# A warm-up for TensorE, and half of the slot inputs turned by VectorE and a trip through DRAM

## The chip, the cores and the metric

The kernel runs on one core of one Trainium2 chip. A core has five engines that run side by side and wait for each other by semaphores: TensorE (PE in the profile; PEld is its weight load), VectorE (DVE), ScalarE (ACT), GpSimd (POOL) and SyncE (SP), which here issues all the DMAs. All data is float32. The metric is the device time of one execution in microseconds. Before the change the median of three runs is 435.57 us (434.58 to 435.74).

## The reference, cut to what matters

Two batches of 1024 tokens with 256 features pass through four blocks, each added to its input: an attention on a short context, a grouped feed-forward, a second attention with sigmoid weights, and a soft mixture of experts with 8 experts of 128 slots (1024 slots in all). The change touches the start of the program and the last block:

```python
xn = rms_norm(x, gamma_x)
se = rms_norm(slot_embeds, gamma_slot)
logits = jnp.einsum('bsd,etd->bset', xn, se)
dispatch = jax.nn.softmax(logits, axis=1)
slots = jnp.einsum('bsd,bset->betd', xn, dispatch)
h = jax.nn.gelu(slots @ w1, approximate=False)
processed = h @ w2
combine = jax.nn.softmax(logits.reshape(b, s, e * t), axis=-1)
out = jnp.einsum('bnd,bsn->bsd', processed.reshape(b, e * t, d), combine)
```

The slots are a weighted mean of the tokens for each slot (`dispatch`), the experts are one two-layer network on each slot, and `combine` brings the results back to the tokens.

## The kernel before, in words

The program is written with tiles whose waits a framework places. Parts under `tc.manual_schedule` keep the order of the text on the engines named (`IN_ORDER` is DVE and PE); elsewhere a scheduler with its own estimates orders each engine, and `keep_in_program_order` pins single instructions to their place in the text. Every DMA is issued by SP, in one order, and each DMA takes the next of eight semaphores, so that one cannot be issued before the DMA eight places ahead of it has landed.

**Start.** SP loads the first group of feed-forward weights in five pieces (`load_group(0, (1, 1, 2, 2, 2))`, L802), and PE multiplies the two weight matrices of the group with each other (`product(0)`, L820: 16 matmuls, 32 records of the trace, since a float32 matmul leaves two). Meanwhile POOL fills the constants: `ident`, `ones`, zeros, and the biases' `b2z`. Then come the key and value products of the first attention (`pk`, `pv`, `pwk`, `pvw`), and for each quarter of the tokens `weigh(q)` (scores `psc`, softmax on DVE and ACT) and `attend(q)` (L1056: PE turns the weights, `pat`, ACT copies them to `atT`, PE multiplies, `po`).

**Gather.** For each batch b, `gather(b, c)` (L398) sums the tokens for the 128 slots of chunk c, c from 0 to 7: 8 matmuls into a PSUM bank (`psl`, L390), the last column of which is the sum of weights. DVE takes its reciprocal (`rz`, L409) and scales the chunk (`sl`, L411). `turn_slots(b, c)` has PE turn the chunk, two transposes of 128x128 against `ident` (`pst`, L420), so that features lie on partitions; for each pair of chunks `slots_out` (L427) has DVE copy the turned pair out of PSUM and scale it by gamma_x (L428, one instruction for each half of the features) into `slT`. Seven of the eight turns stand in the gather, one chunk late; the last stands in `hidden`.

**Turns of the exponentials.** The combine step needs the exponentials `ec` with slots on partitions. `turn(q, h)` (L279) turns half of them for a quarter q of the tokens: four DVE transposes of 32x32 squares (L297) into `tr`, then 16 DMAs (L306) that put the squares in their places, back into `ec`. Batch 0 has the quarters 0 and 1, batch 1 the quarters 2 and 3. Before, turns (0,0), (0,1) and (1,0) stand in the gather of batch 0 at c = 1, 2 and 6, turn (1,1) in `processed(0)`, and the four of batch 1 in its gather at c = 0, 2, 4 and 6. In the gather of batch 0 DVE also has three of the eight additions `less` (L376), the rest of which POOL does.

**Hidden, processed, combined.** `hidden(b)` (L470) multiplies `slT` by w1 by Strassen's scheme in Winograd's form, with seven products of 512-column quadrants for each j from 0 to 3 (`pmh`, L476). Its right sides are sums of quadrants of `slT` made by `sum_slots` (L450); its left sides were made by POOL in `sum_weights` (L438) in the memory that held `seT`. The products go through eight PSUM banks; DVE adds them (L517 to L533), ACT applies the Gelu (L486). `processed` (`pp`) and `combined` (`pc`) are further such schemes, both through L547. `first_sums` of batch 1 stands in `processed(1)` and is the first reader of the turned `ec` there.

The same trip by way of DRAM that the change uses is already there as `turned_by_square` (L155): DVE transposes by squares (L134), one DMA of 512 KB writes them to DRAM, four DMAs of 128 KB bring them back to their places (L159, L161). It turns the slot embeddings and the inputs of the second attention, and `in_order` (L166) views such a tile with its columns in order.

Of the kernel before, what the change touches and what calls it, by code (L numbers as in the profile page):

```python
# [9 lines left out]
FP = mybir.dt.float32  # L10
AF = mybir.ActivationFunctionType
ALU = mybir.AluOpType
# [3 lines left out]
P = 128  # L16
B = 2
S = 1024
D = 256
# [33 lines left out]
def tile_kernel(  # L53
# [29 lines left out]
    def bank(name, side=0):  # L83
        return ps[side].tile([P, 512], FP, tag="bank", name=name)

    ident = const.tile([P, P], FP, name="ident")
    make_identity(nc, ident)
    ones = const.tile([P, P], FP, name="ones")
    nc.gpsimd.memset(ones, 1.0)
    zero = const.tile([P, 1], FP, name="zero")  # L90
    nc.gpsimd.memset(zero, 0.0)

# [30 lines left out]
    def transposed(src, dst, name, side=0, out=nc.any.tensor_copy):  # L123

        for c in range(DC):
# [2 lines left out]
                nc.tensor.transpose(pt[:, ts(t, P)], src[:, t, ts(c, P)], ident)  # L128
            out(dst[:, c, :], pt)

    def squares(src, tr, late=False):

        for t in range(QT):
            turn = nc.vector.transpose(  # L134
                tr[:, :, :, t, :].rearrange("p r c n -> p c r n"),
                src[:, t, 0:D].rearrange("p (c r n) -> p c r n", c=DC, r=R4),
            )
            if late:
                tc.keep_in_program_order(turn)

# [14 lines left out]
    def turned_by_square(src, dst, tr, name, late=False):  # L155

        squares(src, tr, late)
        by_row = dram.tile([P, R4, DC * QN // R4], FP, name=f"d_{name}")
# [221 lines left out]

    slTs, prs, pts, sls, hss, m12s = {}, {}, {}, {}, {}, []

    pzs = {}

    def gather_from(b, c, tiles):
        if c not in pzs:
# [11 lines left out]
    def gather(b, c):  # L398

        if b == 0 and c == 0:  # L400

            for tiles in (range(4), range(4, ST)):
                for i in range(3):
                    gather_from(b, i, tiles)
        elif b > 0 or c > 2:
            gather_from(b, c, range(ST))
        pz = pzs.pop(c)
        rz = stat.tile([P, 1], FP, tag="rz", name=f"rz_{b}_{c}")
        nc.vector.reciprocal(rz, pz[:, D : D + 1])  # L409
        sl = pools["m12"].tile([P, D], FP, tag="sl", name=f"sl_{b}_{c}", bufs=2)  # L410
        nc.vector.tensor_scalar(sl, pz[:, 0:D], rz, None, ALU.mult)  # L411
        sls[c] = sl

    def turn_slots(b, c):

        if c % 2 == 0:
            pts[c // 2] = bank(f"pst_{b}_{c // 2}", 1)
        pt = pts[c // 2]
        for dc in range(DC):
            nc.tensor.transpose(  # L420
                pt[:, ds(dc * 2 * P + (c % 2) * P, P)], sls[c][:, ts(dc, P)], ident
            )
        if c % 2 and c < EC - 1:
            for dc in range(DC):
                slots_out(b, c // 2, dc)

    def slots_out(b, c2, dc):  # L427
        nc.vector.tensor_scalar(  # L428
            slTs[b][:, dc, ts(c2, 2 * P)], pts[c2][:, ts(dc, 2 * P)], gx[:, dc : dc + 1],
            None, ALU.mult,  # L430
        )


# [4 lines left out]
    def sum_weights():  # L438
        m1s = m12s[0]
        a11, a12 = m1s[:, 0, 0:512], m1s[:, 1, 0:512]  # L440
        a21, a22 = m1s[:, 0, 512:], m1s[:, 1, 512:]
        st = const.tile([P, DC, NSLOT], FP, tag="seT", name="m1_sums")
        s1, s2, s4 = st[:, 0, 0:512], st[:, 0, 512:], st[:, 1, 0:512]
        nc.gpsimd.tensor_tensor(s1, a21, a22, ALU.add)
        nc.gpsimd.tensor_tensor(a21, a11, a21, ALU.subtract)
        nc.gpsimd.tensor_tensor(s2, s1, a11, ALU.subtract)
        nc.gpsimd.tensor_tensor(s4, a12, s2, ALU.subtract)
        lefts.extend([a11, a12, s4, a22, s1, s2, a21])

    def sum_slots(b):  # L450

        x = slTs[b]
        b11, b12, b21, b22 = x[:, 0, 0:512], x[:, 0, 512:], x[:, 1, 0:512], x[:, 1, 512:]

        t0, t1_ = (
            keep[b].tile([P, QT, XW], FP, tag=f"xh_{i}", name=f"sl_sums_{b}_{i}").rearrange(
                "p t d -> p (t d)"
            )
            for i in range(2)
        )  # L460
        t1, t2, t4 = t0[:, 0:512], t0[:, 512:1024], t1_[:, 0:512]
        slots_out(b, EC // 2 - 1, 0)
        nc.vector.tensor_tensor(t1, b12, b11, ALU.subtract)
        slots_out(b, EC // 2 - 1, 1)
        nc.vector.tensor_tensor(t2, b22, t1, ALU.subtract)
        nc.vector.tensor_tensor(b12, b22, b12, ALU.subtract)
        nc.vector.tensor_tensor(t4, b21, t2, ALU.subtract)
        rights[b] = [b11, b21, b22, t4, t1, t2, b12]

    def hidden(b):  # L470


        def alone(i, j):
            to = bank(f"pmh_{b}_{j}_{i}", nb[0] % 2)
            nb[0] += 1
            nc.tensor.matmul(  # L476
                to,
                lhsT=lefts[i][:, ts(j, P)],
                rhs=slTs[b][:, i, 0:512] if i < 2 else rights[b][i],
                start=True,  # L480
                stop=True,
            )
            return to

        def gelu(h):
            nc.scalar.activation(h, h, AF.Gelu)  # L486

        NU = OC // 2

        with tc.manual_schedule(engines=IN_ORDER):  # L490
            p1s = [alone(0, 0)]
            turn_slots(b, EC - 1)
            p1s.append(alone(0, 1))
            p2 = alone(1, 0)
            sum_slots(b)
        hs = {}

        def begin(j):

            for g in range(2):  # L500
                for u in range(2):
                    fc = j + u * NU
                    if fc % 2 == 0:
                        hss[b, g, fc // 2] = keep[b].tile(
                            [P, 2, 512], FP, tag=f"lg_{4 * g + fc // 2}", name=f"mh_{b}_{g}_{fc}"
                        )
            hs[j] = [
                hss[b, g, (j + u * NU) // 2][:, j % 2, :] for g in range(2) for u in range(2)
            ]
            nc.scalar.copy(hs[j][0], p1s[j])  # L510

        begin(0)
        for j in range(NU):
            h11, h21, h12, h22 = hs[j]
            p5 = alone(4, j)
            p6 = alone(5, j)
            nc.vector.tensor_tensor(h12, h11, p6, ALU.add)  # L517
# [12 lines left out]
            nc.vector.tensor_tensor(h11, h11, p2, ALU.add)  # L530
            gelu(h11)
            p3 = alone(2, j)
            nc.vector.tensor_tensor(h12, h12, p3, ALU.add)  # L533
            gelu(h12)
            if j + 2 < NU:
                p1s.append(alone(0, j + 2))

    nb = [0]

# [220 lines left out]
    with (  # L760
# [135 lines left out]
        with tc.tile_pool(name="p0", bufs=1) as p0, tc.tile_pool(name="a0", bufs=2) as a0:  # L896
# [156 lines left out]
                )  # L1053
                ats[q] = at

            def attend(q):  # L1056
# [5 lines left out]
                nc.scalar.copy(atT, pat)  # L1062
                for i in range(2):
                    po = bank(f"po0_{q}_{i}")
                    for k in range(2):
# [266 lines left out]
    for u in range(1, B * ST + 2):  # L1332
# [24 lines left out]
        ms[:, 0 : DC * FF].rearrange("p (c n) -> p c n", c=DC),  # L1357
        ms[:, DC * FF :].rearrange("p (c n) -> p c n", c=OC),
    ]
    nc.sync.dma_start(out=ms, in_=m12_in)  # L1360
    for b in range(B):
        slTs[b] = pools["slp"].tile([P, DC, NSLOT], FP, tag="slT", name=f"slT_{b}")
        with tc.manual_schedule(engines=(IN_ORDER | {mybir.EngineType.SP}, ACT_ORDER)[b]):
# [93 lines left out]
```

## Time and profile before

| | |
|---|---|
| median of three runs | 435.57 us |
| profiled execution, time / span | 435.35 / 433.5 us |
| PE / DVE / ACT / POOL busy | 423.7 / 335.0 / 111.8 / 81.3 us |
| first matmul starts | 3.83 us |
| gather of batch 0 (`psl`), `hidden(0)` starts | 222.06 us, 251.50 us |
| gather of batch 1, `hidden(1)` starts | 326.05 us, 355.50 us |
| last work on the chain ends | DVE L711, 430.43 us |

The 1.85 us between time and span lie outside the recorded instructions. Times in the text are microseconds from the start of the span. "x32" counts records, and a float32 matmul has two. The list of waits names the engine and line that waited, what released it, the total, the number of times and the longest; the chain of waits follows the work back from the end of the execution; the timeline gives start and duration, and in brackets the idle time before an instruction and what ended it.

### The profile page before, as it was taken

The page shows a single profiled execution, that of the slowest core. Times are in us where ns is not written, and L with a number is a line of the kernel's source. Part 1 is how long each engine was busy: PE and PEld are TensorE (multiplying, and loading weights), DVE is VectorE, ACT ScalarE, POOL GpSimd, SP SyncE. Part 2 cuts the span into 40 slices and gives each one's busy share as a digit, 9 for nine tenths or more (in the row PEclk, how much of TensorE's full clock was granted, in tenths as well). Part 3 has the DMA queues.
Part 4 walks back from the last instruction along what each step waited for, and adds up shares of the span by engine and source line. Part 5 has one row for each costly group of instructions (what it writes and reads, how often), then busy time and mean ns, then how long its engine had stood idle before and what let it go on. Part 6 is the DMA issues. An engine that isn't in the chain of part 4 may idle for free.

```text
span 433.5 us, 6357 instructions
## 1 busy us (share of the span) xinstructions
PE 423.7 (98%) x2328; PEld 314.6 (73%) x2328; DVE 335.0 (77%) x751; ACT 111.8 (26%) x210; POOL 81.3 (19%) x81
## 2 busy tenths in 40 slices
PE   6999999999999999999999999999999999999996
PEld 5778888888644445444468854799998874499996
DVE  0576989899866787998777997995994669795956
ACT  1212143203244441333570536400000003520000
POOL 3011331325122111200886920000000000000000
PEclk9999999999999999999999999999999999999999
DMA  8997496520443432321044664041013666500002
GB/s 276 406 421 301 160 369 271 195 98 2 145 147 105 110 48 30 48 30 21 0 144 126 98 99 73 0 72 28 0 38 81 97 98 91 85 2 1 2 2 98
DMA packets 96641, 47.86 MB, mean 110 GB/s; under 512 B 86625, under 2 KB 91873, under 8 KB 95201
## 3 DMA queue, kind: packets, MB, share of 16 engines
q1 hardware_dynamic: 96610, 47.46, 39.4%
q8 instruction: 18, 0.29, 0.3%
q14 instruction: 13, 0.11, 0.1%
HBM read 31.70 MB, written 5.25 MB: 85 GB/s over the span
## 4 chain that ended last, share of the span: by engine, by line
PE 84%; DVE 11%; POOL 1%; ACT 1%; issue 1%; DMA 1%; DVEq 0%; ACTq 0%
PE psl L390 13%; PE pp L547 12%; PE pc L547 12%; PE pmh L476 11%; PE pmt L820 10%; PE pl L245 7%; PE pq L1204 3%; PE pf L1218 3%; PE po L879 2%; DVE b2z L851 2%; PE psg L1275 2%; PE poT L1307 2%; DVE lg L253 1%; PE psc L1029 1%; DVE hn_f L780 1%
## 5 line engine op out<-in xcount | busy, mean ns | idle before, releaser
L820 PE MATMUL pmt<-wg 128*128 128x256 f32 x256 | 59.8, 392 | 3.8 <-DMA wg<-in_wff_dram 3.8
L390 PE MATMUL psl<-xh,lg 128*128 128x258 f32 x256 | 58.0, 380 | 0.0
L820 PEld LDWEIGHTS pmt<-wg 128*128 128x128 f32 x256 | 50.0, 197 | 10.9 <-DMA wg<-in_wff_dram 3.8
L245 PE MATMUL pl<-seT,xhT 128*128 128x512 f32 x128 | 56.1, 594 | 0.2 <-DVE rmax L264 0.2
L390 PEld LDWEIGHTS psl<-xh,lg 128*128 128x128 f32 x256 | 47.6, 190 | 7.0 <-issue 0.5
L245 PEld LDWEIGHTS pl<-seT,xhT 128*128 128x128 f32 x128 | 24.1, 190 | 29.2 <-issue 25.7
L376 POOL TENSOR_TENSOR lg<-lg,mb 128x1024 f32<-128x1024 f32 x13 | 33.2, 2597 | 26.8 <-ACT mb L192 25.3
L547 PEld LDWEIGHTS pp<-ms,mh 128*128 128x128 f32 x256 | 29.4, 192 | 1.0 <-issue 1.0
L547 PE MATMUL pp<-ms,mh 128*128 128x128 f32 x256 | 29.7, 276 | 0.0
L268 ACT ACTIVATE ec<-lg,nm 128x1024 f32<-128x1024 f32 x16 | 18.4, 1149 | 39.7 <-DVE nm L253 39.7
L851 DVE SCALAR_TENSOR_TENSOR b2z<-wg,fr,b2z 128x256 f32<-128x256 f32 x48 | 24.6, 514 | 0.4
L486 ACT ACTIVATE mh<-mh 128x512 f32<-128x512 f32 x32 | 19.3, 628 | 20.3 <-DVE mh L520 18.7
L476 PE MATMUL pmh<-slT,ms 128*128 128x512 f32 x48 | 24.2, 592 | 0.0
L547 PE MATMUL pp<-m_sums,mh 128*128 128x128 f32 x192 | 22.1, 275 | 0.0
L547 PE MATMUL pc<-pr,ec 128*128 128x128 f32 x192 | 22.1, 275 | 0.0
L547 PEld LDWEIGHTS pp<-m_sums,mh 128*128 128x128 f32 x192 | 21.8, 192 | 0.0
L547 PEld LDWEIGHTS pc<-pr,ec 128*128 128x128 f32 x192 | 21.8, 192 | 0.0
L1284 ACT ACTIVATE sg<-psg 128x512 f32<-128x512 f32 x32 | 16.5, 602 | 18.6 <-PE psg L1275 18.6
L379 ACT ACTIVATE lg<-lg 128x1024 f32<-128x1024 f32 x16 | 16.1, 1045 | 16.6 <-POOL lg L376 16.6
L297 DVE STREAM_TRANSPOSE tr<-ec 128x512 f32<-128x512 f32 x32 | 19.8, 678 | 0.0
L558 DVE TENSOR_TENSOR mh<-mh,mh 128x1024 f32<-128x1024 f32 x16 | 18.5, 1220 | 1.5 <-PE pp L547 1.5
L547 PE MATMUL pc<-pr_sums,ec 128*128 128x128 f32 x160 | 18.5, 275 | 0.0
(189 smaller groups left out, 678.9 us busy)
## 6 DMA issues: line engine op xcount, KB each, us to landing
wg<-in_wff_dram SPq DMA_DIRECT2D x6, 2048.0 KB, 15.0
ec<-tr SPq DMA_DIRECT2D x128, 64.0 KB, 2.3
xT<-in_xT_dram SPq DMA_DIRECT2D x4, 512.0 KB, 13.2
x<-in_x_dram SPq DMA_DIRECT2D x4, 512.0 KB, 14.8
wg<-in_wff_dram SPq DMA_DIRECT2D x2, 1024.0 KB, 11.3
d_a<-tr_a SPq DMA_DIRECT2D x4, 512.0 KB, 2.6
hTa<-d_a SPq DMA_DIRECT2D x16, 128.0 KB, 2.8
xhT<-tr_m SPq DMA_DIRECT2D x64, 32.0 KB, 2.0
```

Of the source, the lines that this page charges most:

```text
L245: nc.tensor.matmul(pl, lhsT=xhTs[q][:, dc, ts(t, P)], rhs=in_order(seT[:, n], dc), start=(dc == 0), stop=(dc == DC - 1),)
L268: nc.scalar.activation(ecs[q][:, :, t, :], lg.rearrange("p (h n) -> p h n", h=2), AF.Exp, bias=nm[:, 1:2], scale=-1.0, accum_out=zcs[b][:, ...
L297: ins = nc.vector.transpose(tr[:, :, :, t, :].rearrange("p r c n -> p c r n"), half[:, t, :].rearrange("p (c r n) -> p c r n", c=EC // 2, ...
L376: engine.tensor_tensor(lgs[b][s], lgs[b][s], mbs[b], ALU.add)
L390: nc.tensor.matmul(pz[:, 0:XW], lhsT=lgs[b][s][:, ts(c, P)], rhs=xhs[b * QB + s // QT][:, s % QT, :], start=(s == 0), stop=(s == ST - 1),)
L476: nc.tensor.matmul(to, lhsT=lefts[i][:, ts(j, P)], rhs=slTs[b][:, i, 0:512] if i < 2 else rights[b][i], start=True, stop=True,)
L486: nc.scalar.activation(h, h, AF.Gelu)
L547: nc.tensor.matmul(to, lhsT=left(k, m), rhs=right[:, k, :], start=(k == 0), stop=(k == QT - 1),)
L558: nc.vector.tensor_tensor(dst, x, y, op)
L820: nc.tensor.matmul(pm[:, ts(hc, D)], lhsT=w1g[:, oc, ts(hc, P)], rhs=w2g[:, oc, :], start=(oc == 0 and hc == 0), stop=(oc == OC - 1 and hc ...
L851: nc.vector.scalar_tensor_tensor(acc, weights[g][1][:, oc, :], b1s[:, g, oc : oc + 1], acc, ALU.mult, ALU.add)
L1284: nc.scalar.activation(sg[:, j, :], psgs[j], AF.Tanh, scale=0.5 * DH1**-0.5)
```

## The change

- `ones` is filled by DVE in place of POOL, ahead of `ident`, and PE begins with seven matmuls `ones` by `ones` of 128x128 into a bank that nobody reads (`busy`).
- For chunks 0 to 3 of each batch `gather` scales by the reciprocal and by gamma in one DVE instruction (gamma_x now lies along the free dimension, `gx_row`, loaded by a DMA of its own into the memory of `m1_sums`), DVE transposes the chunk by squares, and after chunk 3 the four go by way of DRAM into the first half of `slT`. Chunks 4 to 7 are turned by PE as before. `slT` is now two views, the first in the order of squares, and readers of the first half go through `in_order` or `by_square`.
- The turns of the exponentials stand elsewhere: (0,0) and (0,1) at c = 3 and 4, (1,0) in `hidden(0)` after j = 1, and in batch 1 (2,0), (2,1), (3,0), (3,1) at c = 0, 4, 5 and 6. The gather of batch 1 now keeps the text's order on DVE, PE and SP.
- `attend` is split: the turn of the first quarter's weights (`turn_weights(0)`) stands ahead of `weigh(1)`.

```diff
+    ones = const.tile([P, P], FP, name="ones")
+    nc.vector.memset(ones, 1.0)
+    busy = bank("busy")
+    for _ in range(7):
+        nc.tensor.matmul(busy[:, 0:P], lhsT=ones, rhs=ones, start=True, stop=True)
     ident = const.tile([P, P], FP, name="ident")
     make_identity(nc, ident)
-    ones = const.tile([P, P], FP, name="ones")
-    nc.gpsimd.memset(ones, 1.0)
...
+    def square(rows, tr, t):
+        return nc.vector.transpose(
+            tr[:, :, :, t, :].rearrange("p r c n -> p c r n"),
+            rows.rearrange("p (c r n) -> p c r n", c=DC, r=R4),
+        )
...
+        if c >= QT:
+            nc.vector.tensor_scalar(sl, pz[:, 0:D], rz, None, ALU.mult)
+            sls[c] = sl
+            return
+
+        nc.vector.scalar_tensor_tensor(sl, pz[:, 0:D], rz, gx_row[0], ALU.mult, ALU.mult)
+        if c == 0:
+            trs_sl[b] = pools["md"].tile(
+                [P, R4, DC, QT, SQ], FP, tag="rmax", name=f"tr_sl_{b}"
+            )
+        square(sl, trs_sl[b], c)
+        if c == QT - 1:
+            from_squares(trs_sl[b], slTs[b][0], f"sl_{b}")
...
-        if c % 2 and c < EC - 1:
+        if c == EC - 3:
...
-        nc.vector.tensor_tensor(t1, b12, b11, ALU.subtract)
+        nc.vector.tensor_tensor(by_square(t1), by_square(b12), b11, ALU.subtract)
...
-                rhs=slTs[b][:, i, 0:512] if i < 2 else rights[b][i],
+                rhs=in_order(slTs[b][0], i) if i < 2 else rights[b][i],
...
-            nc.vector.tensor_tensor(h12, h11, p6, ALU.add)
+            ins = nc.vector.tensor_tensor(h12, h11, p6, ALU.add)
+            if b == 0 and j == 2:
+                tc.keep_in_program_order(ins)
...
                 p1s.append(alone(0, j + 2))
+            if b == 0 and j == 1:
+                turn(1, 0, True)
...
             product(1)
+            turn_weights(0)
             weigh(1)
             attend(0)
...
+    m1_sums.append(const.tile([P, DC, NSLOT], FP, tag="seT", name="m1_sums"))
+
+    gx_row.append(m1_sums[0][:, 1, 512 : 512 + D])
+    nc.sync.dma_start(out=gx_row[0], in_=gammas[0].partition_broadcast(P))
     nc.sync.dma_start(out=ms, in_=m12_in)
...
-                if c > 0:
+                if c > QT:
                     turn_slots(b, c - 1)
...
-                if b == 0 and c in (1, 2, 6):
-                    turn(c // 4, c // 2 % 2 if c < 4 else 0)
-                if b == 1 and c % 2 == 0:
-                    turn(QB + c // 4, c // 2 % 2, True)
+                if b == 0 and c in (3, 4):
+                    turn(0, c - 3)
+                if b == 1 and c in (0, 4, 5, 6):
+                    turn(*{0: (2, 0), 4: (2, 1), 5: (3, 0), 6: (3, 1)}[c])
```

As built, four other places move: a copy `bs` (128x256, for the first group's bias) goes from ACT to DVE, POOL makes `ident` after it has cleared `b2z`, most of the bias row `pp` of group 0 goes behind `pk` on PE, and in `hidden(0)` at j = 2 DVE's addition of p2 (L530) goes ahead of that of L520.

More of the change, by code (lines that the diff above doesn't have):

```diff
@@ L129, in transposed @@
             out(dst[:, c, :], pt)
+    def square(rows, tr, t):
[3 more added lines that the diff above has]
+        )
     def squares(src, tr, late=False):
         for t in range(QT):
[L134 to L137, printed above, removed]
+            turn = square(src[:, t, 0:D], tr, t)
             if late:
@@ L157, in turned_by_square, with from_squares @@
         squares(src, tr, late)
+        from_squares(tr, dst, name)
+    def from_squares(tr, dst, name):
         by_row = dram.tile([P, R4, DC * QN // R4], FP, name=f"d_{name}")
@@ L381, in tile_kernel @@
     slTs, prs, pts, sls, hss, m12s = {}, {}, {}, {}, {}, []
-    pzs = {}
+    pzs, trs_sl, gx_row, m1_sums = {}, {}, [], []
     def gather_from(b, c, tiles):
@@ L410, in gather @@
         sl = pools["m12"].tile([P, D], FP, tag="sl", name=f"sl_{b}_{c}", bufs=2)
-        nc.vector.tensor_scalar(sl, pz[:, 0:D], rz, None, ALU.mult)
-        sls[c] = sl
+        if c >= QT:
[10 more added lines that the diff above has]
+            from_squares(trs_sl[b], slTs[b][0], f"sl_{b}")
     def turn_slots(b, c):
@@ L428, in slots_out @@
         nc.vector.tensor_scalar(
-            slTs[b][:, dc, ts(c2, 2 * P)], pts[c2][:, ts(dc, 2 * P)], gx[:, dc : dc + 1],
-            None, ALU.mult,
+            slTs[b][1][:, dc, ts(c2 - 2, 2 * P)], pts[c2][:, ts(dc, 2 * P)],
+            gx[:, dc : dc + 1], None, ALU.mult,
         )
@@ L441, in sum_weights @@
         a21, a22 = m1s[:, 0, 512:], m1s[:, 1, 512:]
-        st = const.tile([P, DC, NSLOT], FP, tag="seT", name="m1_sums")
+        st = m1_sums[0]
         s1, s2, s4 = st[:, 0, 0:512], st[:, 0, 512:], st[:, 1, 0:512]
@@ L450, in sum_slots, with by_square @@
     def sum_slots(b):
-        x = slTs[b]
-        b11, b12, b21, b22 = x[:, 0, 0:512], x[:, 0, 512:], x[:, 1, 0:512], x[:, 1, 512:]
+        x, y = slTs[b]
+        b11, b21 = in_order(x, 0), in_order(x, 1)
+        b12, b22 = y[:, 0, :], y[:, 1, :]
+        def by_square(v):
+            return v.rearrange("p (t i n) -> p t i n", t=QT, i=R4)
         t0, t1_ = (
@@ L466, in sum_slots @@
         nc.vector.tensor_tensor(b12, b22, b12, ALU.subtract)
-        nc.vector.tensor_tensor(t4, b21, t2, ALU.subtract)
+        nc.vector.tensor_tensor(by_square(t4), b21, by_square(t2), ALU.subtract)
         rights[b] = [b11, b21, b22, t4, t1, t2, b12]
@@ L1054, in weigh, with turn_weights @@
                 ats[q] = at
-            def attend(q):
+            atTs = {}
+            def turn_weights(q):
                 atf = ats[q].rearrange("p g j -> p (g j)")
@@ L1062, in attend @@
                 nc.scalar.copy(atT, pat)
+                atTs[q] = atT
+            def attend(q):
+                if q not in atTs:
+                    turn_weights(q)
+                atT = atTs[q]
                 for i in range(2):
@@ L1359, in tile_kernel @@
     ]
+    m1_sums.append(const.tile([P, DC, NSLOT], FP, tag="seT", name="m1_sums"))
+    gx_row.append(m1_sums[0][:, 1, 512 : 512 + D])
+    nc.sync.dma_start(out=gx_row[0], in_=gammas[0].partition_broadcast(P))
     nc.sync.dma_start(out=ms, in_=m12_in)
     for b in range(B):
-        slTs[b] = pools["slp"].tile([P, DC, NSLOT], FP, tag="slT", name=f"slT_{b}")
-        with tc.manual_schedule(engines=(IN_ORDER | {mybir.EngineType.SP}, ACT_ORDER)[b]):
+        slT = pools["slp"].tile([P, 2, NSLOT], FP, tag="slT", name=f"slT_{b}")
+        slTs[b] = [
+            slT[:, 0].rearrange("p (i c t n) -> p i c t n", i=R4, c=DC, t=QT),
+            slT[:, 1].rearrange("p (c n) -> p c n", c=DC),
+        ]
+        with tc.manual_schedule(engines=IN_ORDER | {mybir.EngineType.SP}):
             if b == 0:
```

## The prediction

> **What bounds the kernel now.** I read busy time first, then the list of waits, the chain of waits, and last the timeline of the stages that are touched.
>
> ```profile
> PE 423.7 (98%) x2328; PEld 314.6 (73%) x2328; DVE 335.0 (77%) x751; ACT 111.8 (26%) x210; POOL 81.3 (19%) x81
> ```
>
> PE is busy for 423.7 of 433.5 us. A busy PE need not be at its peak, so the idle rest and the pace matter. The waits of PE itself are few:
>
> ```profile
> PE pmt L820 <- DMA wg<-in_wff_dram: 3.8, 1, 3.8
> ...
> PE pwk L986 <- ACT vblk L975: 1.0, 1, 1.0
> ...
> PE po L1067 <- ACT atT L1062: 0.7, 1, 0.7
> ...
> PE po L1067 <- DVE x L886: 0.5, 1, 0.5
> ```
>
> With 0.2 us elsewhere these are 6.2 us; about 3 us lie behind the last matmul. So work taken from PE shortens the run, wherever no other engine becomes late. The chain of waits for the gather of batch 0 (start, length) shows PE without a gap:
>
> ```profile
> 232.53 0.44 PE pst L420 x4
> 232.96 3.49 PE psl L390 x16
> 236.45 0.22 PE pst L420 x2
> ...
> 251.28 0.22 PE pst L420 x2
> 251.50 0.86 PE pmh L476 x2
> 252.58 23.35 PE pmh L476 x54
> ```
>
> A chunk's gather is 3.49 us, the two transposes of a chunk 0.22. The pace, from the timeline of the first product and of the second, with equal work:
>
> ```profile
> 3.83 9.80 PE L820 MATMUL pmt<-wg 128*128 128x256 f32 x32 [3.83 <-DMA wg<-in_wff_dram]
> ...
> 28.02 7.07 PE L820 MATMUL pmt<-wg 128*128 128x256 f32 x32
> ```
>
> The first takes 2.7 us more. Starts of its records are 0.43 us apart up to 9.11 and 0.215 after: PE runs at half its pace for 5.3 us after its first matmul (the page's PEclk row shows 9 there all the same).
>
> **Part 1, the warm-up.** DVE's `ones` can begin where the other engines' first work does, 0.72; POOL's fill of that size took 0.20; so PE starts near 1.05. Seven matmuls of 128 columns are 14 records; at half pace a 256-column record is 0.43, a 128-column one 0.21, so they last 3.0 us, to 4.05, against data at 3.83 (0.2 lost). If PE speeds up 5.35 us after its first work, as it did, that is at 6.4 in place of 9.2. Then 5.5 records fit in 4.05 to 6.4 and the other 26.5 take 0.215 each: 12.1. The weights allow that: SP's issues wait for landings, which puts the third to fifth piece at 6.6, 8.7 and 10.0, and two matmul groups (16 records) after 8.7 end at 12.1 too. So 13.63 becomes 12.15: 1.5 us, and I take 1.4. Bounds: no sooner pace gives minus 0.2; data forbid more than 1.5.
>
> [...]
>
> Does this gain reach the end? Behind the product stand `pk` (wk0s lands at 12.14, its issue at 3.84 plus 8.3), `pv` (wv0s 14.8, needed at 15.7), `psc` (xT 18.6, needed at 24.7), and the second product (second half of its weights at 26.0, needed at 26.6). All hold, the last by 0.6 us only; the next weights land 4 us ahead and later loads wait for buffers that come free sooner too. PE's order `pp` after `pk` changes no sum. The wait of `pwk` for `vblk` stays, since ACT still starts after `pv`.
>
> **Part 2, the first attention.** `pat` ahead of `psc` takes the 0.7 us wait for `atT` from PE, but `mx` on DVE comes 0.44 later (the time of `pat`), and the chain runs through DVE from 36.91 to 69.48, where PE waits 0.5 for L886. On DVE: `mx` 0.44 later, the idle 0.82 before L1075 gone, the moved copy `bs` 0.4 more (ACT's took 0.38): about 0. Bounds minus 0.5 to plus 0.4; I take 0. `ident` is ready near 3.3 instead of 1.4; DVE has nothing else before 10.9, and PE needs it at 36.
>
> **Part 3, the transposes.** Per batch, PE loses four pairs of L420: 4 x 0.22 = 0.87 us, 1.75 in both. DVE loses four L428 (0.48) and gains four L134 of 0.41 and four times the difference of a two-operand scaling (L851, 0.51) and L411 (0.48): nothing in sum. SP gains the `gx_row` DMA, 0.36, ahead of the load of w1 and w2, so that POOL's sums end at 235.7 instead of 235.3, used from 250.6. `gx_row` itself, 128 KB issued at 222.1, is needed at 229.5.
>
> The price is the trip through DRAM, with rows from its other use:
>
> ```profile
> d_a<-tr_a SPq DMA_DIRECT2D x4, 512.0 KB, 2.6
> hTa<-d_a SPq DMA_DIRECT2D x16, 128.0 KB, 2.8
> ```
>
> The four issues on the way back took 1.73. Batch 0: chunk 3 is gathered at 236.0 (no transposes before it), the chunk is scaled and turned at 237.1, SP is free, so the data is back at 237.1 + 2.65 + 1.73 + 2.8 = 244.3. The first `pmh` wants it at 251.50 - 0.87 = 250.6; 6 us of cover. Batch 1: turn (2,0) is ahead on SP.
>
> ```profile
> 332.73 43.86 SPq L306 DMA_DIRECT2D ec<-tr  x64
> ```
>
> That is 0.67 an issue, 10.8 a turn. With 0.45 more DVE work ahead it begins at 333.2 and ends at 343.95, though chunk 3 is ready at 341.1. Then 2.65 to 3.8 (the `d_se` trip), 1.73, and 2.8 to 3.3: back at 351.1 to 352.8. Needed at 355.50 - 0.87 = 354.6; cover 1.8 to 3.5 us. If it fails, each us late is a us of the run.
>
> Behind it SP holds three turns, 32.2 us: from 348.4 to 349.7 they end at 380.6 to 381.9, land 2.3 later, 383 to 384.2, where before the last was issued at 376.6. Their first reader of the last half is the third sum of `first_sums(1)` at 383.38 - 0.87 = 382.5, so DVE may stall 0.5 to 1.7 us there. DVE then idles 1.02 anyway before L558's next group, and that group's first result stands 1.6 ahead of PE's p7: cost 0, at most 0.5.
>
> [...]
>
> **Part 4, the turns moved.** In the gather of batch 0 DVE loses one turn (2.48), but (0,0) and (0,1) now run from 237.1 with L376 between them (1.6 to 2.4 each), and chunk 5 is scaled near 246.7, just when PE wants to transpose it; I charge 0.1. Turn (1,0) goes into `hidden(0)`:
>
> ```profile
> 265.45 0.68 DVE L533 TENSOR_TENSOR mh<-mh,pmh 128x512 f32<-128x512 f32 x1
> 267.46 0.69 DVE L517 TENSOR_TENSOR mh<-mh,pmh 128x512 f32<-128x512 f32 x1 [1.33 <-PE pmh L476]
> ...
> 272.61 0.69 DVE L517 TENSOR_TENSOR mh<-mh,pmh 128x512 f32<-128x512 f32 x1 [0.56 <-PE pmh L476]
> ```
>
> The gap of 1.33 plus the other 0.56 hold 1.9 of the turn's 2.4 us, so the adds of j = 3 are some 0.4 late. PE's banks still come free in time (the latest, by ACT's copy, at 272.4 for 273.2), but `pp` starts on the last Gelu with 0.1 to spare: 0.2 lost. Bounds 0 and 1.0 (the 1.04 by which the turn overruns its first gap); I take 0.2. SP does its 16 issues at 267.7 to 278.5, ahead of the stores and of turn (1,1) at 280; read at 304. The four turns of batch 1 leave DVE 0.1 later at its last chunk (355.3 for a transpose at 355.5): 0.
>
> **Sum**, against the profiled execution's own 435.35 (span 433.5 and 1.85 around it; 0.2 under the median): -1.4 + 0 - 1.75 + 0.1 + 0.2 = -2.85, so 432.5; with 0.1 for small new waits, 432.6.
>
> **The rivals.**
> - The warm-up does not pay (full pace tied to something else, or the gain lost to the 0.6 us of cover at the second product): 435.35 + 0.2 - 1.75 + 0.4 = 434.2. For: one trace cannot tell a delay after the first matmul from a point in time. Against: 5.3 us of half pace begin with PE's first work.
> - DVE becomes the bound in the gather of batch 0 and `hidden(0)`: 0.8 more there (1.0 for 0.2), 0.4 more for the late chunks (0.5 for 0.1), 0.4 more in `processed(1)` (0.5 for 0.1): 432.6 + 1.6 = 434.2. For: gaps of 0.27 and 0.68 on DVE there. Against: DVE's work in the gather falls by 2.5.
> - Slower: the trip through DRAM in batch 1 queues behind the turns' small packets. Decisive from 3 us late, a landing at 357.5. If both legs took the 8.3 us of wk0s, when the DMA engines were full: 343.95 + 8.3 + 1.73 + 8.3 = 362.3, 7.7 late; 432.6 + 7.7 = 440.3. Against: the turns keep the DMA engines 0.66 busy, and L306 lands in 2.3 us (longest 4.1).
>
> **How the numbers follow.** Forecast 0.68 (own range 431.6 to 433.6), no warm-up 0.14, DVE 0.10, slower 0.08. A measurement tells some 0.3%, 1.3 us, from no change, that is below 434.3. The forecast and half of the first two rivals are under it: 0.68 + 0.12, faster 0.80; their other half, and a late trip that only eats the gain: same 0.13; slower 0.07. The range leaves out the slow case and what lies beyond the bounds: 431.2 to 434.8.
>
> **What would show it.** Right: `busy` near 1.05, the first product's end near 12.2; L420 with 16 records instead of 32; `hidden` 0.87 nearer to its gather's start in both batches; no wait of `pmh` on a DMA. Wrong: a wait of `pmh` for `slT<-d_sl`; waits of `pp` on ACT or of L558 on `ec<-tr` over 1 us; records 0.43 apart up to 9.

## The result and the profile after

| | before | after |
|---|---|---|
| median, 8 executions of each on one chip | 435.65 us (434.16 to 436.20) | 433.79 us (433.51 to 434.35) |
| ratio, with its 95% interval | | 0.9969 [0.9955, 0.9982] |
| profiled execution, time / span | 435.35 / 433.5 us | 433.77 / 432.0 us |

The changed kernel is faster by 1.9 us in the medians, 1.6 in the profiled executions and some 1.35 by the ratio (0.31%). The forecast of 432.6 missed by 1.2 us; its range holds the time, but the gain is between half and seven tenths of the 2.75 us foreseen. Two later comparisons of the same kernel gave 0.9981 [0.9972, 0.999] and 0.9965 [0.9952, 0.9977].

PE's busy time has hardly moved (423.5 us from 423.7), although 16 records of transposes are gone: 14 records of warm-up are new (3.4 us), and the line of the first product is busy for 58.0 us in place of 59.8. So busy time says little; the list of waits says more (total, times, longest, in us):

```profile
PE pst L442 <- DVE sl L423: 1.2, 1, 1.2
PE busy L92 <- DVE ones L89: 1.0, 1, 1.0
...
PE pmt L851 <- DMA wg<-in_wff_dram: 0.6, 1, 0.6
PE pt_f L133 <- DVE e L1072: 0.6, 1, 0.6
```

The wait for the first weights (3.8) is now one of 1.0 for `ones` and one of 0.6 for the third piece of the weights; that for `atT` (0.7) is gone, and one of 0.6 for DVE's `e` stands in the attention instead (`pt_f`). No `pmh` waits for a DMA. But the first line is new: the transpose of a slot chunk waits 1.2 us for DVE's scaling. The chain of waits of the changed kernel shows the place (start, length, in us), the gather of batch 0 that was PE without a gap before:

```profile
240.99 2.40 DVE tr L308 x4
243.39 2.62 DVE lg L387
...
246.12 0.49 DVE sl L423
...
246.66 0.44 PE pst L442 x2
247.10 3.49 PE psl L401 x16
```

From chunk 3 on, the chain runs through DVE: a turn (L308), an addition `lg` (L387), the scaled chunk, and then PE's transpose, which was wanted at 245.45. Stage by stage, from the two timelines of PE:

| from – to | before | after | change |
|---|---|---|---|
| start – the `po` that waits 0.5 us for DVE | 69.48 | 68.23 | -1.25 |
| to the first `psl` of batch 0 (221.90, 220.66) | 152.42 | 152.43 | 0.0 |
| gather(0), to the first `pmh` | 29.44 | 29.99 | +0.55 |
| hidden(0) and processed(0), to the first `pc` | 49.54 | 49.88 | +0.34 |
| combined(0), to the first `psl` of batch 1 | 25.01 | 25.01 | 0.0 |
| gather(1) | 29.44 | 28.57 | -0.87 |

Gather(1) became shorter by what was foreseen, 0.87 us. Gather(0) should have too, and became longer by 0.55. That is a loss of 1.4 us, and the main question.

### The profile page after: what moved, and what is told of

The parts are those of the page before. It is cut to its first block, busy times and chain, and to the rows that moved or that the text cites. A ratio compares the mean times of both kernels' runs of the same rounds, so it can differ in the third digit from the quotient of the medians.

```text
span 432.0 us, 6378 instructions
## 1 busy us (share of the span) xinstructions
PE 423.5 (98%) x2326; PEld 314.6 (73%) x2326; DVE 336.9 (78%) x753; ACT 111.3 (26%) x209; POOL 81.5 (19%) x80
## 4 chain that ended last, share of the span: by engine, by line
PE 79%; DVE 15%; POOL 1%; DMA 1%; issue 1%; ACT 1%; SPq 0%; DVEq 0%; ACTq 0%
PE pc L578 12%; PE pp L578 11%; PE psl L401 11%; PE pmh L503 10%; PE pmt L851 9%; PE pl L256 7%; PE pq L1244 3%; PE pf L1258 3%; PE po L910 2%; DVE b2z L882 2%; PE psg L1315 2%; PE poT L1347 2%; DVE lg L264 1%; DMA wg<-in_wff_dram 1%; DVE tr L308 1%
## 5 line engine op out<-in xcount | busy, mean ns | idle before, releaser
L851 PE MATMUL pmt<-wg 128*128 128x256 f32 x256 | 58.0, 382 | 0.6 <-DMA wg<-in_wff_dram 0.6
L401 PE MATMUL psl<-xh,lg 128*128 128x258 f32 x256 | 56.8, 380 | 0.0
L851 PEld LDWEIGHTS pmt<-wg 128*128 128x128 f32 x256 | 48.5, 192 | 7.6 <-DMA wg<-in_wff_dram 1.2
L387 POOL TENSOR_TENSOR lg<-lg,mb 128x1024 f32<-128x1024 f32 x13 | 33.2, 2590 | 26.8 <-ACT mb L203 25.3
L308 DVE STREAM_TRANSPOSE tr<-ec 128x512 f32<-128x512 f32 x32 | 19.8, 675 | 0.0
```

Source lines behind the costliest of these rows:

```text
L308: ins = nc.vector.transpose(tr[:, :, :, t, :].rearrange("p r c n -> p c r n"), half[:, t, :].rearrange("p (c r n) -> p c r n", c=EC // 2, ...
L387: engine.tensor_tensor(lgs[b][s], lgs[b][s], mbs[b], ALU.add)
L401: nc.tensor.matmul(pz[:, 0:XW], lhsT=lgs[b][s][:, ts(c, P)], rhs=xhs[b * QB + s // QT][:, s % QT, :], start=(s == 0), stop=(s == ST - 1),)
L851: nc.tensor.matmul(pm[:, ts(hc, D)], lhsT=w1g[:, oc, ts(hc, P)], rhs=w2g[:, oc, :], start=(oc == 0 and hc == 0), stop=(oc == OC - 1 and hc ...
```

## The experiments

Line numbers of the profiles are those of the kernel named. Each ratio is against executions of the kernel before on the same chip.

**What the late chunk waits for.** My first theory was DVE's order: turn (0,1) stands between two additions and delays chunk 5. The rival was the additions themselves. In `less` (L387) DVE makes three of the eight additions of the largest logits of batch 1, and POOL five, both on 128x1024 in SBUF, at the same time. DVE's three from the timelines, first of the kernel before, then of the changed kernel:

```profile
238.70 1.64 DVE L376 TENSOR_TENSOR lg<-lg,mb 128x1024 f32<-128x1024 f32 x1
...
241.64 2.00 DVE L376 TENSOR_TENSOR lg<-lg,mb 128x1024 f32<-128x1024 f32 x1
...
244.51 2.42 DVE L376 TENSOR_TENSOR lg<-lg,mb 128x1024 f32<-128x1024 f32 x1
```

```profile
238.27 2.12 DVE L387 TENSOR_TENSOR lg<-lg,mb 128x1024 f32<-128x1024 f32 x1
...
243.31 2.70 DVE L387 TENSOR_TENSOR lg<-lg,mb 128x1024 f32<-128x1024 f32 x1
...
246.53 2.79 DVE L387 TENSOR_TENSOR lg<-lg,mb 128x1024 f32<-128x1024 f32 x1
```

Two experiments tell the two apart. The first moves the turn:

```diff
-                if b == 0 and c in (3, 4):
-                    turn(0, c - 3)
+                if b == 0 and c in (3, 6):
+                    turn(0, c // 6)
```

> The changed kernel with one edit: in the gather of batch 0 the turn (0,1) stands at c = 6 in place of c = 4. In the changed kernel PE waits 1.20 us for the scaling of chunk 5, and gather to first hidden product takes 29.99 us where 28.6 was predicted. Theory (DVE's order): chunk 5 stands behind a turn of 2.4 us and two additions of 2.1 and 2.7 us; with the turn behind chunk 6 the wait is gone, gather to hidden is 28.6 to 28.8, and the time falls by 1.1 to 1.4 us to 432.4 to 432.7. Rival (the sum of DVE's work in the gather is too much for any order): the wait only moves to chunk 7 or to the sums of the slots, and the time stays within 0.4 us of 433.8.

It measured 434.01 us, ratio 0.9974 [0.9964, 0.9983]: nothing gained. The wait did not go, it moved to 251.68 (1.6 us), inside the hidden layer's first products. The last of the three additions in DVE's timeline of this kernel:

```profile
244.48 2.79 DVE L387 TENSOR_TENSOR lg<-lg,mb 128x1024 f32<-128x1024 f32 x1
```

Without the turn between them the three additions, from 237.88, 241.18 and 244.48, take 2.79 each. The order of DVE's work was not the cause; my first theory fell. The second experiment makes POOL's additions short (on 32 of 1024 columns, so that most of those five tiles goes without it; their exponential is taken at a scale of -0.01):

```diff
+        n = 32 if b == 1 and engine is nc.gpsimd else NSLOT
         engine.tensor_tensor(
-            lgs[b][s], lgs[b][s], mbs[b], ALU.add)
+            lgs[b][s][:, 0:n], lgs[b][s][:, 0:n], mbs[b][:, 0:n], ALU.add
+        )
```

> The changed kernel, but POOL's five additions of batch 1 work on 32 of 1024 columns only, and the exponentials behind them have another scale so that they stay finite: the subtraction of the largest logit is left out there. Theory (a DVE addition from SBUF to SBUF stands still until POOL's current addition ends): DVE's three additions take 1.2 us each, 3.7 in sum instead of 7.6, PE's wait for chunk 5 is gone, gather to hidden 28.6 to 28.8 instead of 29.99. Rival (the DMAs into SBUF or ACT slow them): they stay at 2.1 to 2.8 us and PE's wait stays near 1.2.

One execution took 432.22 us (span 430.4). DVE's additions, untouched by the edit, from its timeline:

```profile
238.15 1.21 DVE L388 TENSOR_TENSOR lg<-lg,mb 128x1024 f32<-128x1024 f32 x1
242.28 1.18 DVE L388 TENSOR_TENSOR lg<-lg,mb 128x1024 f32<-128x1024 f32 x1
243.98 1.22 DVE L388 TENSOR_TENSOR lg<-lg,mb 128x1024 f32<-128x1024 f32 x1
```

No chunk waits, and gather(0) takes 28.6 us. So the addition itself is 1.2 us, and the rest is time in which it stands. POOL's five additions in the changed kernel say for what:

```profile
236.96 2.36 POOL L387 TENSOR_TENSOR lg<-lg,mb 128x1024 f32<-128x1024 f32 x1 [1.54 <-DMA mb<-mrow]
239.28 3.34 POOL L387 TENSOR_TENSOR lg<-lg,mb 128x1024 f32<-128x1024 f32 x1
242.57 2.35 POOL L387 TENSOR_TENSOR lg<-lg,mb 128x1024 f32<-128x1024 f32 x1
244.89 3.35 POOL L387 TENSOR_TENSOR lg<-lg,mb 128x1024 f32<-128x1024 f32 x1
248.20 3.35 POOL L387 TENSOR_TENSOR lg<-lg,mb 128x1024 f32<-128x1024 f32 x1
```

DVE's three end at 240.39, 246.01 and 249.32, each 1.1 us after one of POOL's begins, and it is just these three of POOL's that take 1.0 us longer than the other two. So in these traces the engines take turns, one whole operation each, and an addition of DVE takes 1.2 us alone and 1.6 to 2.8 beside POOL's. What makes them take turns is not shown.

**Can the additions go to one engine?** If all eight go to POOL, no addition of DVE can meet them:

```diff
-        engine = nc.vector if b == 1 and s in (3, 4, 5) else nc.gpsimd
-        engine.tensor_tensor(lgs[b][s], lgs[b][s], mbs[b], ALU.add)
+        nc.gpsimd.tensor_tensor(lgs[b][s], lgs[b][s], mbs[b], ALU.add)
...
         sums(a12, a12, a22, SUB)
+        if b == 0:
+            for s in range(5, ST):
+                dispatch(1, s)
...
-                    if c > 0:
+                    if 0 < c < 6:
                         dispatch(1, c - 1)
-        if b == 0:
-            dispatch(1, ST - 1)
```

> All eight additions of the second batch's largest in GpSimd, none in VectorE; the last three exponentials of them go from the first gather into processed(0), behind the differences of the activations there. The theory (VectorE's additions stand until GpSimd's current operation ends, and the slot tile of the last transposes comes 1.2 us late behind them) expects no wait of TensorE for the slots' chunks in the first gather, 28.6 us from the first gather's start to the first product of the hidden layer (29.99 in the changed kernel, 29.44 before), and 432.4 us (432.0 to 433.0), 1.2 to 1.4 below the changed kernel. The rival (GpSimd's additions, now eight up to about 256 us, slow VectorE's sums of the slots and the hidden layer's first additions as they stretched each other in the gather) expects 433.6 or more, with the loss in hidden(0). That it is the rest of VectorE's order (turn and scaling, not the additions) expects the wait of 1.2 to stay and 433.8.

The rival held, and by more than it said: 437.86 us, ratio 1.0073 [1.0056, 1.009]. The profiled execution is the shortest of the six, 435.72 at a mean granted clock of 1.0 (the share of its full clock that PE was given); the others took 437.0 to 438.9 at 0.991 to 0.995, and what these lost beyond the profiled one is not shown. Gather(0) is 28.6 us as the theory has it, but the wait is now inside hidden(0). From this kernel's list of waits, and DVE's timeline:

```profile
PE pmh L502 <- DVE sl_sums L489: 1.8, 1, 1.8
PE pmh L502 <- DVE sl_sums L491: 1.7, 1, 1.7
```

```profile
248.90 0.48 DVE L422 TENSOR_SCALAR sl<-psl,rz 128x256 f32<-128x256 f32 x1
...
250.51 2.80 DVE L489 TENSOR_TENSOR sl_sums<-slT 128x512 f32<-128x512 f32 x1
...
253.74 2.32 DVE L491 TENSOR_TENSOR sl_sums<-slT,sl_sums 128x512 f32<-128x512 f32 x1
255.99 0.68 DVE L492 TENSOR_TENSOR slT<-slT 128x512 f32<-128x512 f32 x1
```

POOL works until 255.5. The two sums of slots that fall into that time take 2.80 and 2.32 us, the one after it 0.68, on tiles of one size: the same standing, of another operation. The scalings that read PSUM (L422, and L449 at 253.23) keep their 0.48 beside POOL's work, and four transposes of a turn, at 238.40, their 2.48. So it is neither "DVE is slow while POOL works" nor any operation on SBUF: of the kinds that met POOL's work here, it is the one with two inputs from SBUF.

**The additions where POOL makes none.** The other way is to give the last three to DVE in processed(0), where it had waited 5 us for PE (from 292.18 to 297.15 in the changed kernel). The tile of the largest is kept until then, so the allocation of one half of `pr` moves behind them:

```diff
-        engine = nc.vector if b == 1 and s in (3, 4, 5) else nc.gpsimd
+        engine = nc.vector if b == 1 and s >= 5 else nc.gpsimd
...
         sums(a12, a12, a22, SUB)
+        if b == 0:
+            for s in range(5, ST):
+                less(1, s)
+                dispatch(1, s)
+        c21, c22 = processed_half(1)
...
-                if b == 0:
+                if b == 0 and c < 5:
                     less(1, c)
-                    if c > 0:
-                        dispatch(1, c - 1)
-        if b == 0:
-            dispatch(1, ST - 1)
+                if b == 0 and 0 < c < 6:
+                    dispatch(1, c - 1)
```

> The changed kernel, to stand beside the next two on one chip: 433.8 us (433.4 to 434.3), the slots' transposes of the first gather waiting 1.2 to 1.7 us for VectorE.

> GpSimd makes five of the eight additions of the second batch's largest, in the first gather; the other three are VectorE's, and stand in processed(0) in the 5 us in which VectorE waits for TensorE there, their exponentials with them. So no addition of VectorE from SBUF to SBUF meets one of GpSimd, neither in the gather (the changed kernel) nor at the sums of the slots (all eight on GpSimd). The theory expects each of the three to take 1.2 us where it took 2.1 to 2.8, no wait of TensorE for the slots or their sums, 28.5 us from the first gather's start to the hidden layer's first product (30.0 to 30.35 in the changed kernel), processed(0) as long as before, and 432.3 us (431.9 to 432.8). That processed(0) has no room for them (rival) gives back 0.5 to 3 us there, with a wait of its last product for VectorE: 433 to 435.

On one chip the changed kernel measured 433.58 us, ratio 0.9965 [0.9952, 0.9977], and this one 432.03 (431.48 to 432.45), ratio 0.9929 [0.9915, 0.9943]: 1.55 us below the changed kernel and within the 431.9 to 432.8 expected. The timelines of POOL and DVE:

```profile
236.96 11.64 POOL L387 TENSOR_TENSOR lg<-lg,mb 128x1024 f32<-128x1024 f32 x5 [2.04 <-DMA mb<-mrow]
```

```profile
290.30 3.49 DVE L387 TENSOR_TENSOR lg<-lg,mb 128x1024 f32<-128x1024 f32 x3
295.35 4.31 DVE L589 TENSOR_TENSOR pr<-pr,pp 128x512 f32<-128x512 f32 x6 [1.56 <-PE pp L578]
```

DVE's three take 3.49 us together (7.61 in the changed kernel), POOL's five 11.64 (14.59): both engines had paid for meeting. DVE still waits 1.56 us for PE after them, so the room sufficed. Gather(0) takes 28.56 us, 0.88 below the kernel before, as gather(1) does.

**The turn in hidden(0).** It costs the rest of batch 0's loss. Left out:

```diff
-            if b == 0 and j == 1:
-                turn(1, 0, True)
```

> The changed kernel without the turn of exponentials that stands in the first hidden layer (its eight transposes and two copies are left out, so one half of the exponentials of one quarter is not turned). If that turn costs what the prediction gave it, 0.2 us, hidden(0) and processed(0) together take 49.7 us, against 49.88 in the changed kernel and 49.54 before; by the bounds of the prediction 48.9 to 49.9. If the 0.34 us above the kernel before are all the turn's, 49.54 and 433.4 us. TensorE's own transposes take 0.7 to 0.9 us of it in any case, where TensorE is what sets the pace: then 49.0.

From the first `pmh` to the first `pc` it takes 49.54 us, exactly the time before; so the turn costs 0.34. The time of the single execution, 433.57 us, shows little of it, because its gather(0) took 30.44. My expectation was wrong in one thing: a turn is four transposes of DVE and 16 DMAs and has no work on PE, so its last sentence is void. Then I put the turn back into the gather, on top of the kernel with the moved additions, where DVE idles 2 to 3 us at a time (2.24 and 3.02 in its timeline):

```diff
-                if b == 0 and c in (3, 4):
-                    turn(0, c - 3)
+                if b == 0 and c in (3, 4, 6):
+                    turn(*{3: (0, 0), 4: (0, 1), 6: (1, 0)}[c])
...
-            if b == 0 and j == 1:
-                turn(1, 0, True)
```

> The same, and the turn that the change put in hidden(0) back in the first gather, ahead of the seventh chunk's transposes, where VectorE's idle stretches of 2 to 3 us without the additions are. If that turn is what hidden(0) and processed(0) lost (0.34 us), and the gather has room for it, 0.3 below the kernel with the additions alone, 432.0 us (431.6 to 432.5); if the slot tiles come late behind the turn's 2.45 us, a wait of TensorE of 0.5 to 1.5 us for them and 432.5 to 433.5.

Neither outcome: 439.87 us, ratio 1.0114 [1.0096, 1.0132]. From the timelines of DVE and PE, and the table of windows (from:to, length, busy us of PE, PEld, DVE, ACT and POOL, granted clock, DMA share, GB/s):

```profile
253.15 2.49 DVE L308 STREAM_TRANSPOSE tr<-ec 128x512 f32<-128x512 f32 x4 [6.44 <-DMA ec<-tr]
```

```profile
256.27 0.69 PE L442 MATMUL pst<-ident,sl 128*128 128x128 f32 x2 [6.28 <-DVE sl L423]
256.75 3.22 PE L503 MATMUL pmh<-slT,ms 128*128 128x512 f32 x4
```

```profile
250.00:275.00 25.00, 18.73 (x42) 8.58 (x43) 17.30 (x29) 7.47 (x12) 0.00 (x0) 0.86 0.63 94
```

A turn writes one of two `tr` tiles. The third turn must wait until the 16 DMAs of the first have been issued by SP and landed; SP begins them at 240.53, behind the four DMAs of the slots' trip, and takes 21.80 us for the 32 issues of two turns, so the first tile is free at 253.15. DVE stands there for 6.44 us with the last chunk behind it, and PE stands 6.3. That alone does not make up the loss: hidden(0) starts at 248.97, as in the kernel it was added to (248.85), and lasts 32.3 us up to its `pp` in place of 24.4, 7.9 more. The other 1.6 us are pace: the six records right behind the wait take 0.69 and 3.22 us, where the same ones take 0.38 and 1.88 in the kernel it was added to. The granted clock is 0.86 over the 25 us (1.00 in the 30 us before). So behind this gap of 6.3 us PE ran slower, up to 259.80, from where four records take 1.88 again; how short a gap would do the same is not shown.

So DVE's idle stretches were the wrong measure for the turn's place: the limit was the DMA queue and the two tiles. Hidden(0), at 0.34 us, is the cheaper place.

**Why POOL's additions did not come earlier with PE.** The changed kernel reaches the gather 1.24 us earlier, but POOL's first addition starts at 236.96, before at 236.90. It needs the largest of batch 1, which goes through four DMAs of 4 KB, and the load of w1 and w2, 2 MB, is issued ahead of them.

```diff
-    nc.sync.dma_start(out=ms, in_=m12_in)
+    nc.sync.dma_start(out=ms[:, 0 : DC * FF], in_=m12_in[:, 0 : DC * FF])
...
                     spread_by_moves(1)
+                    nc.sync.dma_start(out=ms[:, DC * FF :], in_=m12_in[:, DC * FF :])
```

> The changed kernel with the second half of the 2 MB load of the combined matrices issued after the small transfers of the second batch's largest. If those small transfers are late because they queue behind that load, the broadcast of the largest is there about 1 us earlier and GpSimd's first addition starts near 236.0 in place of 236.96; if something else sets it, it stays at 236.9 to 237.0. The time: the additions and the wait of 1.2 us move together by up to 1 us if GpSimd's start is what sets them, 432.9 us; 433.8 if the broadcast is not late for that reason.

The issues for `max` land after a median of 2.9 us (4.5 in the changed kernel, 3.6 before), and POOL starts at 236.29 where three profiles of the changed kernel show 236.85, 236.93 and 236.96. So the load is part of it: 0.6 of the 1 us, in one execution. The wait of `pst` is 1.0 there, against 1.2 to 1.6, and that execution took 433.24 us. The broadcast `mb` itself landed in 4.2 instead of 3.5 us, beside the second half of the load.

POOL's start sets more than this wait. In the six profiles that have the additions in the changed kernel's order (three of it, those without the hidden turn and with the split load, and the one without the warm-up below), the first `pmh` starts 13.69 to 13.71 us after POOL's first addition, while it starts 29.75 to 30.44 after the first `psl`. In the three of the changed kernel the first `psl` starts at 220.66, 220.28 and 220.26, and the first `pmh` at 250.65, 250.63 and 250.56: what PE gains ahead of the gather is lost in it.

**The two gains at the start.** The changed kernel without the seven matmuls, and the kernel before with them and nothing else:

```diff
-    busy = bank("busy")
-    for _ in range(7):
-        nc.tensor.matmul(busy[:, 0:P], lhsT=ones, rhs=ones, start=True, stop=True)
```

> The changed kernel without the seven warm-up matmuls; all else as it is. Theory (the warm-up works, but the weights' landing caps it): the first product ends near 13.6 instead of 12.81, so the time is 0.8 us more, 434.4 to 434.8. The prediction's own term would make it 1.4 us more, 435.2. Rival (the warm-up does nothing and the start moved by chance): 433.8, with half pace ending at the same time after the span's start.

> The kernel before with the warm-up alone (ones filled by DVE ahead of the identity, seven matmuls). Theory: 0.8 us less than before, 434.6 to 435.0, with the first product's end near 12.8 and a wait of some 0.6 us on the weights' DMA within it. The prediction's own term: 1.4 us less, 434.2. Rival (no effect): 435.6.

They measured 433.98 us, 0.9975 [0.9964, 0.9986], and 434.50, 0.9986 [0.9977, 0.9995]. The warm-up alone makes the kernel before shorter by 0.5 to 0.6 us (434.6 to 435.0 was expected). Taking it out of the changed kernel changes nothing that the times can tell: the 434.4 to 434.8 expected was missed, and the ratio lies among the three of the changed kernel (0.9965 to 0.9981). The profiles show where the gain is made. With the start of the second product and of the `po` that waits 0.5 us for DVE in all four:

| | second product | `po` | between |
|---|---|---|---|
| before | 28.02 | 69.48 | 41.46 |
| new order of the attention alone | 27.86 | 68.91 | 41.05 |
| warm-up alone | 27.38 | 68.86 | 41.48 |
| both (the changed kernel) | 27.19 | 68.23 | 41.04 |

The new order is worth 0.41 and 0.44 us, all between the two. The warm-up is worth 0.64 and 0.67 ahead of the second product, and 0.83 from before to after, since the two profiles without it differ by 0.16 there. The pair shown gained the least: in the ten profiles with both, the second product starts between 26.69 and 27.19. Why not more? The timelines of PE, first of the changed kernel, then of the kernel before with the warm-up alone:

```profile
1.04 3.36 PE L92 MATMUL busy<-ones 128*128 128x128 f32 x14 [1.04 <-DVE ones L89]
4.19 2.48 PE L851 MATMUL pmt<-wg 128*128 128x256 f32 x8
7.29 5.52 PE L851 MATMUL pmt<-wg 128*128 128x256 f32 x24 [0.62 <-DMA wg<-in_wff_dram]
```

```profile
...
9.28 3.72 PE L823 MATMUL pmt<-wg 128*128 128x256 f32 x16 [0.80 <-DMA wg<-in_wff_dram]
```

PE was at full pace from about 5.4 us on (records 0.215 apart from 5.42), 4.4 after its first work where it had been 5.3; that is sooner than the 6.4 I worked with. But it then stood for weights: for the third piece until 7.29 in the one, for the fourth until 9.28 in the other. The product ended at 12.81 and 13.00, against 13.63. In four other executions with the warm-up the first product ran without a gap and took 8.02 us (turn (0,1) late) to 8.29 us (no hidden turn) on the chain of waits, where the second took 6.91. From these lengths, at 0.43 us for a record at half pace and 0.215 at full, an estimate puts full pace at 5.4 to 5.9 us after PE's first work, so the delay varies.

A repeat of the changed kernel:

> The changed kernel once more, to stand beside the others on one chip. Every theory expects 433.8 us (433.4 to 434.3), 1.2 to 1.8 below the kernel before, and again a wait of about 1.2 us of the slots' transposes in the first gather for VectorE.

It measured 433.88 us, 0.9981 [0.9972, 0.999], with a wait of 1.6 us of `pst` and 0.2 for the weights.

## Why the prediction was right or wrong

| step | foreseen | measured |
|---|---|---|
| Part 1, warm-up | -1.4 | -0.83 |
| Part 2, the first attention | 0 | -0.42 |
| Part 3, transposes, both batches | -1.75 | -1.75 |
| Part 4, chunk 5 in gather(0) | +0.1 | +1.43 |
| Part 4, turn in hidden(0) | +0.2 | +0.34 |
| sum | -2.85 | -1.23 |

The measured sum is that of the stages up to the last combine (404.87 to 403.64); some 0.3 us more were saved behind DVE's last instruction (430.43 and 429.21), for a reason that is not shown, and make the span's 1.5.

- **Part 4 is where it failed**, in the sentence "chunk 5 is scaled near 246.7, just when PE wants to transpose it; I charge 0.1". It cost 1.43: gather(0)'s 29.99 less the 28.56 with the additions moved away (1.74 and 1.79 in the two other profiles of the changed kernel). The time was nearly right: the chunk was scaled at 246.6. But PE wanted it at 245.45, since Parts 1 and 2 had brought PE forward by 1.25, and the sentence sets both engines in the times of the kernel before. DVE came forward as well, its turn (0,0) to 235.90 from the 237.1 foreseen, and gave that back in the two additions ahead of the chunk: 2.12 and 2.70 us, where the first two had taken 1.64 and 2.00. The forecast took "1.6 to 2.4 each" over as the price of an addition. They were 1.2 of work and the rest standing behind POOL's operations, and POOL's start, which hangs on a DMA chain, did not come forward (236.90 to 236.96). So the three took 6.06 us before and 7.61 after. The spread of 1.64 to 2.42 for one shape stood in the trace of before.
- The **rival "DVE becomes the bound"** is what happened in gather(0), where the chain now runs through DVE. Its 434.2 us is nearer to the result than the forecast, but its reason, too much work on DVE, is not what the runs show: with its three additions at 1.2 us, DVE had an idle stretch of 2.24 us there and no chunk waited. I gave it 0.10 because "DVE's work in the gather falls by 2.5", a sum of busy time that does not see when an operation may start.
- **Part 1**: full pace did come sooner, at 5.42 us in place of 9.11, and the size of the gain varies. In the pair shown the second product starts 0.83 earlier, in the nine other profiles with the warm-up and the new order 0.96 to 1.33. The third piece of weights, foreseen at 6.6 us, was waited for until 7.29 in the pair shown. What the forecast missed is that this gain does not reach the end: in gather(0) PE meets a time that POOL sets.
- **Part 2** was costed at nothing within -0.5 to +0.4 and gave -0.42, inside the bounds. The chain does run through DVE there, and `mx` comes 0.44 later behind the second product, as foreseen. But from `mx` to the `po` it takes 31.71 us in place of 32.57, 0.86 less, where the forecast's -0.82 and +0.4 make 0.42 less. Which of DVE's instructions saved the rest is not shown. The wait for `atT` that PE lost is not the reason, since PE now waits 0.6 for DVE's `e`.
- **Part 3** held, in gather(1) at once and in gather(0) once the additions were away. The trip through DRAM cost nothing: in batch 1 the way out is issued at 343.60 (foreseen 343.95), the four back from 346.52 to 348.28, they land after 2.9 us at some 351.2, and `pmh` starts at 354.11. `first_sums(1)` stalls 0.67 us on a turn (foreseen 0.5 to 1.7), and PE does not wait for it. So the slower rival, the late trip, did not happen.
- **The turn in hidden(0)** cost 0.34, within its bounds and where the forecast put it, at the last Gelu: the last three Gelus start 0.61 us after the first `pp` in place of 0.27, and the first 64 `pp` take 7.74 us in place of 7.40.
- The **rival "the warm-up does not pay"** had nearly the right time, 434.2. Full pace did come sooner, so its first reason is wrong. The gain was indeed lost, but not at the second product, where it looked: in gather(0).

With the additions out of each other's way the span is 430.2 us; the forecast, less the 1.85 outside, was 430.7. That these are near is partly luck: Part 2 and the end of the program saved 0.7 that the forecast put at nothing, while Part 1 (1.18 in that profile) and the turn in hidden(0) fell short by 0.4.

## What to carry to other kernels

When a change brings one engine forward, list what does not come forward with it: work tied to a DMA chain or to another engine can keep its absolute time (here POOL's first addition, 236.90 and then 236.96), and cover counted in the old times then shrinks by the whole gain. A gain ahead of such work can vanish in it. A row whose durations differ by half for one shape is not a price; find out what the operation stands for before it is added up, and look first for operations with two SBUF inputs on VectorE beside GpSimd's additions: here they stood until the other's current instruction ended (up to 2.8 us for 1.2 of work). Before work is put into an engine's idle stretch, follow its tiles and DMAs too: the turn fitted into VectorE's idle time and cost 7.8 us for want of a buffer.

## What the runs showed of the hardware that I had not expected

- A two-input SBUF operation of VectorE of 1.2 us took 1.6 to 2.8 beside GpSimd's additions, and one of 0.68 took 2.80; the scalings that read PSUM (0.48) and the transposes of a turn (128x512, 0.62 each) kept their time.
- Transfers of 4 KB issued behind a 2 MB load landed after a median of 4.5 us (3.6 in the kernel before); with half of the load issued behind them, after 2.9.
- One wait of PE of 6.3 us cost 7.9 us up to the next stage: the granted clock was 0.86 over the 25 us around it, and the six records behind it took 1.7 to 1.8 times as long.
- From the same filler matmuls, full pace came 4.4 us after PE's first work in one execution and, by an estimate from the length of the first product (8.02 to 8.29 us), 5.4 to 5.9 us after it in four others.
